# Turning tiles on VectorE and through DRAM instead of on TensorE, with a new order of a planned macaron kernel

## The chip, the cores and the metric

The kernel runs on one core of a Trainium2 chip. The metric is the device time of one launch in microseconds, as the median of several runs; lower is better. The five engines of the core (TensorE or PE for matmuls, VectorE or DVE, ScalarE or ACT, GpSimd or POOL, and SyncE or SP, which here issues all DMAs) run their own instruction streams in order and wait for each other by semaphores.

## What is computed

The input x is 8 sequences of 256 tokens with 128 channels. Six residual layers follow each other, each on a layer-normalized x:

```python
x = x + 0.5 * _L0_ffn_ref(_layernorm(x), ...)   # soft mixture of 16 experts x 64 slots
x = x + _L0_attn_ref(_layernorm(x), ...)        # linear attention, 16 heads, elu + 1
x = x + 0.5 * _L0_ffn_ref(_layernorm(x), ...)   # the soft mixture again
x = x + 0.5 * _L1_ffn_ref(_layernorm(x), ...)   # GLU: silu gate, two hidden layers of 512
x = x + _L1_attn_ref(_layernorm(x), ...)        # attention with FAVOR+ random features
x = x + 0.5 * _L1_ffn_ref(_layernorm(x), ...)   # the GLU again
```

The two attentions, cut to what the change touches:

```python
# L0: out is turned before the last product
out = jnp.einsum('bhnd,bhde->bhne', q, kv) * z
out = jnp.einsum('bnc,oc->bno', out, Wproj) + bproj
# L1: 16 heads x 32 features; phi(q) is turned before num and den
xw = jnp.einsum('bhtd,hmd->bhtm', x, proj)
xw = xw - jnp.max(xw, axis=-1, keepdims=True)
phi = jnp.exp(xw) * jnp.exp(-0.5 * x_norm_sq) + EPS
num = jnp.einsum('bhtm,bhmd->bhtd', phiQ, KV)
den = jnp.einsum('bhtm,bhm->bht', phiQ, Ksum)[..., None] + EPS
```

## The kernel before

All data is float32. x stays in SBUF: 16 tiles of 128 tokens, two to each of the 8 sequences (called blocks, b). The blocks form two groups of four; `group` (L1341) takes one group through the six layers. A product contracts over the partitions, so a normalized tile (tokens on partitions) has to be **turned** to channels on partitions before it can be multiplied with a weight matrix.

Such a turn is a `flip` (L365): a TensorE transpose of a 128x128 tile against the identity into PSUM, followed by a copy to SBUF by ScalarE or VectorE (`evacuated`, L368). `transposed` (L431) turns the tiles of a normalized y: two in `dispatch` of the mixture (with an affine copy), two in `linear` (L877, the first attention) and in `favor` (L1153, the second), four in `glu` (L1088, which takes two blocks at a time). `project` (L848) turns linear attention's output `oh`, two tiles. In `favor`, phi(q) of a block is 128 x 1024: eight flips into two banks, whose copies add the 1e-6 of the features (L1263 to L1271); phi(k) gets its 1e-6 by a GpSimd operation (L1248) and isn't turned.

The mixture's `dispatch` already has another way to turn: its exponentials are transposed by VectorE in 32x32 squares within each group of 32 partitions (L638), which suits products on 32 rows of TensorE at a time. It also spills the normalized tile to DRAM with four DMAs (L539) and spreads it back four times (L546). The weights of the 16 experts are fetched through four buffers `we` (L724, with biases at L727).

Nothing is issued in the order in which it is written. `Plan.step` (L88) records each piece of work with its engines, a duration, its reads and writes and its buffers; `Plan.place` (L121) then puts the steps one after the other on the engines, always the one that can start first, ties broken by a key: the TensorE time recorded so far, plus 45000 for the second group, plus 100 times an entry of the table `SHIFTS` (L16) for its part. A part is a stretch of the program that begins at `plan.part()`; a smaller key is more urgent. Buffers, PSUM banks among them (kind `ps`, eight), are handed out at placing. `Plan.issue` (L199) emits the steps by planned start, so each engine's instruction order is fixed by the plan; at run time the engines wait for semaphores. A step's `lag` is extra time until its result is there; `SP` steps have 2000 ns besides.

At the start, `rehearse` (L1372) multiplies the identity with itself 14 times while the first inputs arrive.

Of the kernel before, what the change touches and what calls it, by code (L numbers as in the profile page):

```python
# [13 lines left out]
P = 128  # L14

SHIFTS = (  # L16
    -1319, -1177, -1179, -234, -76, -310, -312, -70, -340, -338, -86, -385, -231, -437, -534,
    -438, -380, -343, -723, -539, -291, -326, -396, -417, -254, -201, -356, -228, -211, -118,
    -511, -528, 144, 18, -78, 96, 75, -486, -259, 398, 0, 22, 12, -318, -46, 57, 46, 221, -64,
    227, -13, -57, -20, 66, -283, -22, -94, -718, 41, 74, -7, -1, -30, 194, 106, 110, 356, 101,  # L20
    795, 48, -539, 265, -702, -346, -646, -82, 303, -155, 294, 80, -220, -817, 147, -4, 170,
    -282, 25, -136, -36, -246, -35, -196, -181, -374, 25, -551, -218, 387, -155, 231, 607, 1155,
    -140, -62, 4, -209, -206, -92, -131, -189, 63, -176, -155, -174, -142, -353, 51, 69, 141,
    108, 115, 76, 41, 9, -98, -166, -94, 27, -93, -88, -393, -168, -31, 130, -13, -218, -78,
    130, 105, 79, -189, -724, 9, 54, -4219, 183, 328, 534, 422, 1394, 826, 581, -128, 608, -159,
    -23, 92, -24, -186, -220, 25, -168, 774, 492, 254, 433, 585, 230, -113, -207, -80, 377,
    -220, 224, -677, 472, -371, -706, -646, -62, -156, -161, -1077, -2, -479, -102, 119, 36,
    -233, -727, -865, -412, -526, -772, -301, 480, 211, 600, -302, -1825, -1528, 438,
)


# [23 lines left out]
class Step:  # L55
    def __init__(self, number, engines, run, table, key):
        self.number, self.engines, self.run, self.table = number, engines, run, table
        self.key = key
        self.needs, self.feeds, self.bufs = set(), [], []
        self.start = self.end = self.engine = None  # L60


class Plan:
# [57 lines left out]
    def place(self):  # L121

        for s in self.steps:
            s.waiting = sum(n.end is None for n in s.needs)
            for n in s.needs:
                n.feeds.append(s)
        names = list(self.LAG)
        free = dict.fromkeys(names, 800)
        port = 0
        slots = {k: [0] * n for k, n in self.slots.items()}  # L130
        able = {e: [] for e in names}
        table = None
        order = []

        def enable(s):
            s.ready = max((n.end + self.LAG[n.engine] + n.lag for n in s.needs), default=0)
            for e in s.engines:
                able[e].append(s)

        for s in self.steps:  # L140
            if not s.waiting:
                enable(s)
        while len(order) < len(self.steps):
            best = None
            for e in names:
                for s in able[e]:
                    at = max(s.ready, free[e])
                    if e == "POOL":
                        at = max(at, port)
                    elif e == "DVE" and s.port:  # L150
                        at = max(at, free["POOL"])
                    short = {}
                    for b in s.bufs:
                        if b.slot is None:
                            short[b.kind] = short.get(b.kind, 0) + 1
                    for kind, n in short.items():
                        times = sorted(t for t in slots[kind] if t is not None)
                        if len(times) < n:
                            at = None
                            break  # L160
                        at = max(at, times[n - 1])
                    if at is None:
                        continue
                    late = self.TABLE if s.table and s.table != table else 0
                    rank = (at, s.key + 4 * late, s.number)
                    if best is None or rank < best[0]:
                        best = (rank, e, s, at, late)
            if best is None:
                raise RuntimeError("no step can start: too few slots")
            _, e, s, at, late = best  # L170
            for f in s.engines:
                able[f].remove(s)
            s.start, s.engine = at, e
            s.end = free[e] = at + s.engines[e] + late
            if s.table:
                table = s.table
            if e == "DVE" and s.port:
                port = s.end
            for b in s.bufs:
                if b.slot is None:  # L180
                    held = slots[b.kind]
                    b.slot = min(
                        (k for k, t in enumerate(held) if t is not None), key=held.__getitem__
                    )
                    held[b.slot] = None
            for b in s.bufs:
                b.left -= 1
                b.last = max(getattr(b, "last", 0), s.end + self.LAG[e] + s.lag)
                if not b.left:
                    slots[b.kind][b.slot] = b.last  # L190
            order.append(s)
            for n in s.feeds:
                n.waiting -= 1
                if not n.waiting:
                    enable(n)
        self.span = max(free.values())
        self.placed = order

    def issue(self, home):  # L199
        for s in self.steps:  # L200
            for b in s.bufs:
                b.home = home
        for s in sorted(self.placed, key=lambda s: (s.start, s.number)):
            s.run(s.engine)


@with_exitstack
def macaron_kernel(ctx: ExitStack, tc: tile.TileContext, i: dict, out: bass.AP):
# [139 lines left out]
    def ps_(*shape):  # L348
        return Buf("ps", (P, *shape))
# [78 lines left out]
        )  # L428
        return y

    def transposed(y, n, affine=False):  # L431

        pt = ps_(n, P)
        yt = Buf("k1" if n == TT else "k2", (P, n * P))

        def turn(_):
            for t in range(n):
# [409 lines left out]

    def project(b, oh, w):  # L848

        pt = ps_(TT, P)  # L850
        ot = Buf("k1", (P, N))

        def turn(_):
            for t in range(TT):
                flip(pt.ap[:, t, :], oh.ap[:, t, :])

        step({"PE": flips(TT)}, turn, [oh], [pt], takes=[ot])
        evacuated(lambda: ot.ap, lambda: pt.ap.rearrange("p t c -> p (t c)"), [pt], [ot], N)
        projected_onto(b, ot, w)

    def projected_onto(b, ot, w):
# [14 lines left out]

    def linear(b):  # L877
        plan.part()
        yt = transposed(norm(b), TT)
        plus_bias(b, loaded["bproj"])  # L880
        pk, pv = ps_(2, N), ps_(TT, D)
        kq = Buf("k4", (P, 2, 2, N))
# [205 lines left out]
    def glu(b, after):  # L1088
# [7 lines left out]
        y = Buf("k2", (P, 2 * TT, D))  # L1096
        for k in range(2):
            norm(b + k, False, y, k * TT)
        yt = transposed(y, 2 * TT)
        h, to = (Buf("comb", (P, 2, 2, 2, N)) for _ in range(2))  # L1100
        t4 = Buf("comb", (P, 4, 512))
        for o in range(NO):
# [49 lines left out]

    def favor(b):  # L1153
        plan.part()
        yt = transposed(norm(b), TT)
        plus_bias(b, loaded["bo"])
        pq, pv = ps_(2, N), ps_(TT, P)

# [80 lines left out]
        for k in (1, 0):  # L1239
            cells = [(phi, k, c) for c in range(4)]  # L1240

            def exps(_, k=k):
                nc.scalar.activation(phi.ap[:, k], phi.ap[:, k], AF.Exp)

            step({"ACT": act(1024) + 20}, exps, cells, cells, table="exp")
            if k:
                def eps(_, k=k):
                    nc.gpsimd.tensor_scalar(  # L1248
                        phi.ap[:, k], phi.ap[:, k], 1.0, 1e-6, ALU.mult, ALU.add
                    )  # L1250

                step({"POOL": 1100}, eps, cells, cells)

        plan.part()


        qt = lambda t: qk.ap.rearrange("p a b n -> p (a b n)").rearrange(
            "p (t c n) -> p t c n", t=TT, c=4
        )[:, t]
        for t in range(TT):  # L1260
            pt = ps_(4, P)

            def turn(_, t=t, pt=pt):  # L1263
                for c in range(4):
                    flip(pt.ap[:, c, :], phi.ap[:, 0, t, ts(c, P)])

            def finish(e, t=t, pt=pt):
                if e == "ACT":
                    nc.scalar.activation(qt(t), pt.ap, AF.Copy, bias=1e-6)
                else:  # L1270
                    nc.vector.tensor_scalar(qt(t), pt.ap, 1e-6, None, ALU.add)  # L1271

            step({"PE": flips(4)}, turn, [(phi, 0, c) for c in range(4)], [pt])
            step({"ACT": act(512), "DVE": dve(512)}, finish, [pt], [(qk, t)])
        pk, pkt = ps_(2, P), ps_(2, P)
        kvm = Buf("k1", (P, 2, P))

# [91 lines left out]
    )  # L1369
    pwarm = ps_(P)  # L1370

    def rehearse(_):  # L1372
        for _ in range(14):
            mm(pwarm.ap, ident, ident, start=True, stop=True)

    key, plan.key = plan.key, -100000
    step({"PE": 6200}, rehearse, [], [pwarm])
# [8 lines left out]
        nc.tensor.engine, nc.scalar.engine, nc.vector.engine, nc.gpsimd.engine, nc.sync.engine,  # L1386
    }
    with tc.manual_schedule(engines=engines):
        plan.issue(home)


# [62 lines left out]
```

## Time and profile before

| | us |
|---|---|
| median of 3 runs | 758.23 (755.57 to 758.31) |
| the profiled execution | 758.05 |
| its span, first to last instruction | 756.3 |
| TensorE's mean granted clock | 0.995 of full speed |

The groups of instructions that matter here, from the view of groups by shape:

| line, engine, what | count | busy us | mean ns |
|---|---|---|---|
| L747 PE, experts' first products | 512 | 121.0 | 385 |
| L1037 PE, GLU hidden layers | 896 | 205.4 | 381 |
| L366 PE, flips of k tiles | 176 | 34.2 | 284 |
| L366 PE, flips of comb tiles (phi(q)) | 64 | 8.5 | 273 |
| L366 PE, flips of sm tiles | 32 | 5.8 | 278 |
| L373 ACT, copies of 128x256 to k | 25 | 9.2 | 373 |
| L375 DVE, copies of 128x256 to k | 15 | 6.1 | 416 |
| L1269 ACT, copies of turned phi(q) | 11 | 6.3 | 597 |
| L1248 POOL, 1e-6 onto phi(k) | 8 | 8.9 | 1116 |

A float32 matmul is two PE instructions (passes), a flip is one. Busy time of PE is the union of intervals in which some pass is in flight, and passes overlap, so a mean duration is not the distance between two of them. The chain of waits is read for that distance: it follows the work that ended last backwards, so each piece in it lasts as long as it held up the end. Rows that the next section rests on are shown there.

### The profile page before, as it was taken

The page shows a single profiled execution, that of the slowest core. Times are in us where ns is not written, and L with a number is a line of the kernel's source. Part 1 is how long each engine was busy: PE and PEld are TensorE (multiplying, and loading weights), DVE is VectorE, ACT ScalarE, POOL GpSimd, SP SyncE. Part 2 cuts the span into 40 slices and gives each one's busy share as a digit, 9 for nine tenths or more (in the row PEclk, how much of TensorE's full clock was granted, in tenths as well). Part 3 has the DMA queues.
Part 4 walks back from the last instruction along what each step waited for, and adds up shares of the span by engine and source line. Part 5 has one row for each costly group of instructions (what it writes and reads, how often), then busy time and mean ns, then how long its engine had stood idle before and what let it go on. Part 6 is the DMA issues. An engine that isn't in the chain of part 4 may idle for free.

```text
span 756.3 us, 15121 instructions
## 1 busy us (share of the span) xinstructions
PE 738.4 (98%) x5884; PEld 619.5 (82%) x5884; DVE 507.1 (67%) x1084; ACT 432.1 (57%) x815; POOL 294.1 (39%) x404
## 2 busy tenths in 40 slices
PE   7899999999999999999999999999999999999998
PEld 5687888998888988889878788958787896687887
DVE  6986976468988689875453537468875676854432
ACT  4968879756974679873373434146447354644321
POOL 7968318622457444743650201424250151201000
PEclk9999999999999999999999999999999999999999
DMA  5453422224340053323521010000000000000001
GB/s 155 130 156 98 137 92 92 91 82 129 82 145 25 1 143 102 122 91 118 181 72 42 1 49 1 1 1 1 2 1 1 1 1 2 1 1 8 8 1 42
DMA packets 29911, 45.53 MB, mean 60 GB/s; under 512 B 5008, under 2 KB 18704, under 8 KB 29840
## 3 DMA queue, kind: packets, MB, share of 16 engines
q1 hardware_dynamic: 29840, 44.57, 19.6%
q8 instruction: 46, 0.75, 0.4%
q14 instruction: 25, 0.20, 0.1%
HBM read 41.41 MB, written 3.15 MB: 59 GB/s over the span
## 4 chain that ended last, share of the span: by engine, by line
PE 88%; POOL 4%; DVE 3%; DMA 1%; issue 1%; ACT 1%; SPq 1%; ACTq 0%; POOLq 0%; DVEq 0%
PE ps L1037 26%; PE ps L747 14%; PE ps L778 8%; PE ps L651 7%; PE ps L819 6%; PE ps L575 5%; PE ps L1137 4%; PE ps L1107 4%; PE ps L1110 4%; PE ps L366 4%; POOL k L411 1%; POOL sm L405 1%; PE ps L1316 1%; PE ps L1216 1%; PE ps L867 1%
## 5 line engine op out<-in xcount | busy, mean ns | idle before, releaser
L747 PE MATMUL ps<-slots,we 128*128 128x256 f32 x512 | 121.0, 385 | 1.9 <-DMA we<-in_We 1.9
L747 PEld LDWEIGHTS ps<-slots,we 128*128 128x128 f32 x512 | 95.3, 192 | 17.3 <-issue 2.6
L1037 PE MATMUL ps<-comb,slots 128*128 128x256 f32 x448 | 102.8, 381 | 0.0
L1037 PE MATMUL ps<-comb,comb 128*128 128x256 f32 x448 | 102.6, 381 | 0.0
L1037 PEld LDWEIGHTS ps<-comb,slots 128*128 128x128 f32 x448 | 83.4, 190 | 14.5 <-issue 2.2
L1037 PEld LDWEIGHTS ps<-comb,comb 128*128 128x128 f32 x448 | 83.7, 190 | 13.1 <-issue 1.4
L373 ACT COPY k<-ps 128x512 f32<-128x512 f32 (+2 forms) x74 | 36.1, 493 | 87.4 <-PE ps L1037 59.8
L630 POOL TENSOR_TENSOR comb<-comb,sm 128x1024 f32<-128x1024 f32 x32 | 60.6, 1900 | 62.3 <-DVE sm L625 49.8
L697 POOL TENSOR_TENSOR comb<-comb,k 128x1024 f32<-128x1024 f32 x32 | 75.4, 2376 | 22.5 <-ACT k L373 18.3
L753 ACT ACTIVATE k<-ps,small 128x256 f32<-128x256 f32 x128 | 55.1, 475 | 45.1 <-PE ps L747 41.5
L1051 DVE TENSOR_TENSOR comb<-ps,k 128x512 f32<-128x512 f32 x48 | 32.8, 687 | 58.0 <-ACT k L373 31.6
L758 DVE SCALAR_TENSOR_TENSOR k<-ps,small,k 128x256 f32<-128x256 f32 x128 | 56.5, 476 | 20.4 <-ACT k L753 19.9
L617 ACT ACTIVATE comb<-comb,sm 128x256 f32<-128x256 f32 x128 | 63.3, 497 | 5.3 <-DVE sm L609 5.1
L575 PE MATMUL ps<-k,seT 128*128 128x256 f32 x256 | 60.9, 383 | 2.1 <-DVE k L592 0.8
L778 PE MATMUL ps<-we,k 128*64 128x128 f32 x1024 | 61.6, 275 | 0.0
L651 PE MATMUL ps<-comb,k 32*128 32x256 f32 x1024 | 61.4, 387 | 0.0
L778 PEld LDWEIGHTS ps<-we,k 128*64 128x64 f32 x1024 | 55.4, 137 | 7.3 <-issue 3.3
L819 PE MATMUL ps<-slots,comb 128*128 128x129 f32 x512 | 60.4, 276 | 0.0
L403 POOL TENSOR_SCALAR sm<-sm 128x2 f32<-128x2 f32 x52 | 10.1, 194 | 129.0 <-DVE sm L397 118.6
L1059 ACT ACTIVATE comb<-comb 128x512 f32<-128x512 f32 x48 | 30.2, 630 | 51.3 <-DVE comb L1051 51.0
L819 PEld LDWEIGHTS ps<-slots,comb 128*128 128x128 f32 x512 | 58.7, 192 | 1.0 <-issue 0.9
L651 PEld LDWEIGHTS ps<-comb,k 32*128 32x128 f32 x1024 | 52.8, 189 | 6.4 <-issue 2.6
(146 smaller groups left out, 1316.5 us busy)
## 6 DMA issues: line engine op xcount, KB each, us to landing
we<-in_We SPq DMA_DIRECT2D x64, 384.0 KB, 3.9
k<-y SPq DMA_DIRECT2D x64, 128.0 KB, 2.7
y<-k SPq DMA_DIRECT2D x64, 32.0 KB, 1.9
we<-in_bd SPq DMA_DIRECT2D x64, 32.0 KB, 3.6
comb<-in_h2T SPq DMA_DIRECT2D x4, 256.0 KB, 6.9
slots<-in_h1T SPq DMA_DIRECT2D x4, 256.0 KB, 4.5
out<-x SPq DMA_DIRECT2D x8, 128.0 KB, 1.7
x<-in_x SPq DMA_DIRECT2D x3, 256.0 KB, 5.1
```

The source lines that it names most:

```text
L373: nc.scalar.copy(dst(), src())
L575: mm(pl.ap[:, j, :], seT[:, 2 * u + j].rearrange("p k s -> p (k s)"), yt.ap, start=True, stop=True,)
L617: nc.scalar.activation(ex.ap[:, 4 * h + j, :], comb.ap[:, 4 * h + j, :], AF.Exp, bias=mx.ap[:, j : j + 1], accum_out=mx.ap[:, 4 + j : 5 + j],)
L630: nc.gpsimd.tensor_tensor(ex.ap[:, part], ex.ap[:, part], mx.ap[:, 8:12].unsqueeze(2).to_broadcast([P, 4, N]), ALU.mult,)
L651: mm(po.ap, yr.ap[rows, c, :], ex.ap[rows, :, 32 * c : 32 * c + 32], start=(c == 0), stop=(c == N // 32 - 1), tile_position=(32 * a, 0),)
L697: nc.gpsimd.tensor_tensor(raw, raw, mb.ap.unsqueeze(1).to_broadcast([P, 4, N]), ALU.subtract)
L747: mm(pe.ap[:, m, :], we.ap[:, ts(2 * m + c, P)], sl.ap[:, j, k, :, 0:S], start=True, stop=True,)
L753: nc.scalar.activation(ga.ap, pe.ap[:, 0, :], AF.Gelu, bias=bg[:, e, c : c + 1])
L758: nc.vector.scalar_tensor_tensor(ht.ap[:, c, :], pe.ap[:, 1, :], bu[:, e, c : c + 1], ga.ap, ALU.add, ALU.mult,)
L778: mm(po.ap[S * k : S * k + S, q, :], hts[k].ap[:, c, ts(q, S)], wes[k].ap[:, ts(4 + c, P)], start=(c == 0), stop=(c == 1), tile_position=( ...
L819: mm(po.ap[:, t, 0 : D + 1], comb.ap[:, j, ts(t, P)], eo()[:, j, q, 0 : D + 1], start=(j == 0), stop=(j == NJ - 1),)
L1037: mm(bank.ap[:, o], w(k)[:, c, ts(o, P)], rhs().rearrange("p (c n) -> p c n", c=2)[:, c, :], start=(start and o + c == 0), stop=(stop and ...
```

## The change

A new helper, `squares_turned`, turns a piece without TensorE. VectorE transposes it in place in 32x32 squares. One DMA writes the whole piece to a DRAM tile. Four more, one for each group of 32 destination partitions, read the squares back so that each lands where the full transpose wants it; what is moved is runs of 32 floats. It replaces the flips of y in `linear`, `favor` and `glu` (`transposed` with `squares=True`), of linear's output in `project`, and of phi(q) in `favor`. `dispatch` keeps its flips. As no copy is left that could add 1e-6 to phi(q), GpSimd now does it for both phi(k) and phi(q).

`Plan.place` notes where a TensorE step that takes a fresh PSUM bank is planned to start more than 700 ns after TensorE became free, and `Plan.issue` puts identity products into that step's bank ahead of it, one for each 224 ns beyond 300. `SHIFTS` is a new table. In the built program TensorE has 50 identity products (14 of them the old ones); SP issues 497 DMAs.

```diff
 SHIFTS = (
-    -1319, -1177, -1179, -234, -76, -310, -312, -70, -340, -338, -86, -385, -231, -437, -534,
...
+    -1764, -4181, -1024, -349, -26426, -5062, -382, -2111, -1130, -497, 116, -518, -159, 162,
...
 )
...
         self.key = key
         self.needs, self.feeds, self.bufs = set(), [], []
         self.start = self.end = self.engine = None
+        self.idle = 0
 
 
 class Plan:
...
             for f in s.engines:
                 able[f].remove(s)
             s.start, s.engine = at, e
+            before = free[e]
             s.end = free[e] = at + s.engines[e] + late
             if s.table:
                 table = s.table
...
             for b in s.bufs:
                 if b.slot is None:
                     held = slots[b.kind]
+                    if e == "PE" and b.kind == "ps" and not s.idle:
+                        since = max(before, min(t for t in held if t is not None))
+                        s.idle, s.bank = at - since, b
                     b.slot = min(
                         (k for k, t in enumerate(held) if t is not None), key=held.__getitem__
                     )
...
         self.span = max(free.values())
         self.placed = order
 
-    def issue(self, home):
+    def issue(self, home, idle):
+
         for s in self.steps:
             for b in s.bufs:
                 b.home = home
         for s in sorted(self.placed, key=lambda s: (s.start, s.number)):
+            if s.idle > 700:
+                idle(s.bank, int((s.idle - 300) / 224))
             s.run(s.engine)
 
 
...
         )
         return y
 
-    def transposed(y, n, affine=False):
-
+    def squares_turned(z, n, cells, dst, out):
+
+
+        flat = lambda: z()
+        there = dram.tile([P, n // 32, 32], F32, tag=f"t{len(turns)}", name=f"t{len(turns)}")
+        turns.append(there)
+        step({"DVE": 58 + 1.07 * n}, lambda _: nc.vector.transpose(z(), z()), cells, cells)
+
+        def spill(_):
+            nc.sync.dma_start(there.rearrange("p k j -> p (k j)"), z())
+
+
+        def place(_):
+            squares = there.rearrange("(a i) (t f) j -> f i t a j", a=4, f=4)
+            for f in range(4):
+                nc.sync.dma_start(
+                    dst()[32 * f : 32 * f + 32].rearrange("p (t a j) -> p t a j", a=4, j=32),
+                    squares[f],
+                )
+
+        step({"SP": 475}, spill, cells, [there.name], lag=1.5 * n)
+        step({"SP": 2000}, place, [there.name], out, lag=2.5 * n)
+
+    turns = []
+
+    def transposed(y, n, affine=False, squares=False):
+
+        yt = Buf("k1" if n == TT else "k2", (P, n * P))
+        if squares:
+            squares_turned(
+                lambda: y.ap[:, 0:n].rearrange("p t d -> p (t d)"), n * P,
+                [(y, t) for t in range(n)], lambda: yt.ap, [yt],
+            )
+            return yt
         pt = ps_(n, P)
-        yt = Buf("k1" if n == TT else "k2", (P, n * P))
 
         def turn(_):
             for t in range(n):
...
 
     def project(b, oh, w):
 
-        pt = ps_(TT, P)
         ot = Buf("k1", (P, N))
-
-        def turn(_):
-            for t in range(TT):
-                flip(pt.ap[:, t, :], oh.ap[:, t, :])
-
-        step({"PE": flips(TT)}, turn, [oh], [pt], takes=[ot])
-        evacuated(lambda: ot.ap, lambda: pt.ap.rearrange("p t c -> p (t c)"), [pt], [ot], N)
+        squares_turned(
+            lambda: oh.ap.rearrange("p t d -> p (t d)"), N, [oh], lambda: ot.ap, [ot]
+        )
         projected_onto(b, ot, w)
 
     def projected_onto(b, ot, w):
...
 
     def linear(b):
         plan.part()
-        yt = transposed(norm(b), TT)
+        yt = transposed(norm(b), TT, squares=True)
         plus_bias(b, loaded["bproj"])
         pk, pv = ps_(2, N), ps_(TT, D)
         kq = Buf("k4", (P, 2, 2, N))
...
         y = Buf("k2", (P, 2 * TT, D))
         for k in range(2):
             norm(b + k, False, y, k * TT)
-        yt = transposed(y, 2 * TT)
+        yt = transposed(y, 2 * TT, squares=True)
         h, to = (Buf("comb", (P, 2, 2, 2, N)) for _ in range(2))
         t4 = Buf("comb", (P, 4, 512))
         for o in range(NO):
...
 
     def favor(b):
         plan.part()
-        yt = transposed(norm(b), TT)
+        yt = transposed(norm(b), TT, squares=True)
         plus_bias(b, loaded["bo"])
         pq, pv = ps_(2, N), ps_(TT, P)
 
...
                 nc.scalar.activation(phi.ap[:, k], phi.ap[:, k], AF.Exp)
 
             step({"ACT": act(1024) + 20}, exps, cells, cells, table="exp")
-            if k:
-                def eps(_, k=k):
-                    nc.gpsimd.tensor_scalar(
-                        phi.ap[:, k], phi.ap[:, k], 1.0, 1e-6, ALU.mult, ALU.add
-                    )
-
-                step({"POOL": 1100}, eps, cells, cells)
+            def eps(_, k=k):
+                nc.gpsimd.tensor_scalar(
+                    phi.ap[:, k], phi.ap[:, k], 1.0, 1e-6, ALU.mult, ALU.add
+                )
+
+            step({"POOL": 1100}, eps, cells, cells)
 
         plan.part()
 
-
-        qt = lambda t: qk.ap.rearrange("p a b n -> p (a b n)").rearrange(
-            "p (t c n) -> p t c n", t=TT, c=4
-        )[:, t]
-        for t in range(TT):
-            pt = ps_(4, P)
-
-            def turn(_, t=t, pt=pt):
-                for c in range(4):
-                    flip(pt.ap[:, c, :], phi.ap[:, 0, t, ts(c, P)])
-
-            def finish(e, t=t, pt=pt):
-                if e == "ACT":
-                    nc.scalar.activation(qt(t), pt.ap, AF.Copy, bias=1e-6)
-                else:
-                    nc.vector.tensor_scalar(qt(t), pt.ap, 1e-6, None, ALU.add)
-
-            step({"PE": flips(4)}, turn, [(phi, 0, c) for c in range(4)], [pt])
-            step({"ACT": act(512), "DVE": dve(512)}, finish, [pt], [(qk, t)])
+        squares_turned(
+            lambda: phi.ap[:, 0].rearrange("p t c -> p (t c)"), TT * 512,
+            [(phi, 0, c) for c in range(4)],
+            lambda: qk.ap.rearrange("p a b n -> p (a b n)"), [(qk, t) for t in range(TT)],
+        )
         pk, pkt = ps_(2, P), ps_(2, P)
         kvm = Buf("k1", (P, 2, P))
 
...
     )
     pwarm = ps_(P)
 
+    def idle(bank, n):
+        for _ in range(n):
+            mm(bank.home["ps"][bank.slot][:, 0:P], ident, ident, start=True, stop=True)
+
     def rehearse(_):
-        for _ in range(14):
-            mm(pwarm.ap, ident, ident, start=True, stop=True)
+        idle(pwarm, 14)
 
     key, plan.key = plan.key, -100000
     step({"PE": 6200}, rehearse, [], [pwarm])
...
         nc.tensor.engine, nc.scalar.engine, nc.vector.engine, nc.gpsimd.engine, nc.sync.engine,
     }
     with tc.manual_schedule(engines=engines):
-        plan.issue(home)
+        plan.issue(home, idle)
 
 
 def kernel(**inputs):
```

## The prediction

> **What bounds the kernel now.** I read the busy times first, then the chain that ended last, then windows with the granted clock, then the groups by form and the DMA issues.
>
> ```profile
> PE 738.4 (98%) x5884; PEld 619.5 (82%) x5884; DVE 507.1 (67%) x1084; ACT 432.1 (57%) x815; POOL 294.1 (39%) x404
> ...
> PE 88%; POOL 4%; DVE 3%; DMA 1%; issue 1%; ACT 1%; SPq 1%; ACTq 0%; POOLq 0%; DVEq 0%
> ```
>
> TensorE is busy for 738.4 of 756.3 us and is 88% of the chain; no other engine passes 67%. Between 60 us and the tail TensorE idles only some 6 us. So time is TensorE work: what leaves TensorE leaves the span, if no new wait takes its place. The windows show the only stretches in which its clock drops:
>
> ```profile
> 37.00:44.00 7.00, 6.42 (x68) 5.56 (x69) 5.61 (x8) 3.75 (x12) 7.00 (x7) 0.76 0.38 107
> 66.00:72.00 6.00, 6.00 (x23) 4.71 (x22) 2.88 (x7) 3.99 (x7) 6.00 (x4) 0.77 0.02 7
> ```
>
> Columns: stretch, its length, busy us of PE, PEld, DVE, ACT, POOL, then clock, DMA share, GB/s. From 72 us on the clock is 1.00.
>
> **Part 1: flips that leave TensorE.** The order of instructions of both programs has 272 flips before and 128 after. The 144 that go: linear 8 calls x (2 + 2), favor 8 x (2 + 8), glu 8 x 4. Their price where TensorE is dense is read in the chain of waits (start, us, what):
>
> ```profile
> 474.33 1.02 PE ps L366 x8
> ...
> 617.38 1.09 PE ps L366 x10
> ```
>
> That is 128 and 109 ns each (the groups' mean of 284 ns is pipelined latency and would overstate it). 144 x 109 to 128 ns = 15.7 to 18.4 us; I take **-17 us**. After 60 us four waits of TensorE ended at a flip, 3.9 us together; two of them, on a normalized tile (L411, 1.5) and on linear's output (L960, 1.0), may be of the removed kind: -2.5 at best, and I count **-1**.
>
> With the flips go their evacuations: 24 of 256 columns (373 ns on ACT, 416 on DVE) and 24 of 512 (about 590 and 690), some 23 us over two engines with room. Nothing on the path.
>
> **Part 2: what comes instead.** 40 calls of squares_turned: 24 of 256 elements a partition, 8 of 512 (glu), 8 of 1024 (phi(q)). Each is one VectorE transpose, one DMA to DRAM, four DMAs back.
>
> VectorE has the instruction already: 1236 ns for 1024 elements. Scaled, 620 for 512; 256 lies between 310 and its 416 ns copy, I take 340. Sum 8 x 1.24 + 8 x 0.62 + 24 x 0.34 = 23 us, about what the evacuations gave back: VectorE stays near 67%. GpSimd gets the 1e-6 of phi(q): 8 x 1.05 us (row L1248), at 39%. Both are hidden by TensorE's 98%; they cost only as latency inside a turn, below.
>
> The DMA rows:
>
> ```profile
> k<-y SPq DMA_DIRECT2D x64, 128.0 KB, 2.7
> y<-k SPq DMA_DIRECT2D x64, 32.0 KB, 1.9
> ...
> out<-x SPq DMA_DIRECT2D x8, 128.0 KB, 1.7
> ```
>
> The spill of 256 elements is the same transfer as out<-x: 1.7 us. For 1024 I add 384 KB at some 290 GB/s (128 packets of 1 KB of out<-x start within 0.44 us): 3.0 us; for 512, 2.1.
>
> The place is what before does not show: each of its four DMAs writes pieces of 32 floats, 128 B, so 1,024, 2,048 or 4,096 pieces a turn. SP issues such DMAs in 0.42 us (k<-y) to 0.59 (y<-k), so the fourth is issued 1.3 to 1.8 us in, and lands some 2.2 to 2.7 later: 4.2 us if the pieces themselves cost little. What does a piece cost? **Lower end:** the trace's packet records have 13 ns for a 128 B packet (those of projT), 27 for 512 B, 46 for 1 KB; over 16 DMA engines 0.8 ns a piece, 3.3 us for phi(q). **Upper end:** within one y<-k the 64 packets start 4.2 ns apart: 17 us for phi(q). Here a rule speaks against the change. The Trainium skill, "VectorE: DVE Perf Modes", section on the three transpose paths, calls a plain DMA that transposes by access pattern 19 times slower than the crossbar's 1309 ns for a 128x128 tile and sends such turns to TensorE; "DMA: Bandwidth & Descriptors", specifications, wants at least 512 B apiece. Taken by bytes (24.9 us for 32 KB), phi(q)'s 512 KB would cost about 400 us, and the kernel would be several times slower. But the rule's tile moves 16,384 single elements, 1.5 ns each; here VectorE has turned the squares, and 32 floats travel together. By pieces the rule gives 4,096 x 1.5 = 6.2 us. That lies near the row's lower end, so I take **1.6 ns**: 1.6, 3.3 and 6.6 us of transfer, the first hidden under the issues. Place, from first issue to landing: 4.2, 5.3 and 8.3 us.
>
> Now the cover. I counted the TensorE work that the new order puts between the last producer and the first reader of each turn, at the paces of the chain (16 expert products of 256 columns 3.46 us, and so on), and set against it the turn's latency by rows, with about 0.15 us per hand-over:
> - linear's y, 8 turns: add 0.86, statistics 0.89, root 1.08, apply 0.90, turn 0.34, spill 1.7, place 4.2, hand-overs 0.9 = 10.9 us; cover 13.0 to 27.5.
> - linear's output, 8: division 0.95, turn 0.34, spill 1.7, place 4.2, hand-overs 0.6 = 7.8; cover 10.6 to 13.2.
> - favor's y, 8: as linear's, 10.9; cover 12.4 and more.
> - glu, 8: add 0.42, statistics 1.8, root 1.2, apply 1.8, turn 0.62, spill 2.1, place 5.3, hand-overs 0.9 = 14.1; cover 14.5, 15.6, 15.9, 17.2, the rest 19.9 and more.
> - phi(q), 8: four DVE groups of 1.55, table load 1.28, two exps of 1.05, two eps of 1.05 (the first beside an exp), turn 1.24, spill 3.0, place 8.3, hand-overs 0.9 = about 24; cover 24.7, 25.0, 25.3, 26.7, 27.3, 28.2, 29.2, 70.8.
>
> So every turn is covered, the tight ones by 0.3 to 3 us. The sums have no queueing in them: VectorE serves two groups of blocks, and a We fetch of 384 KB (3.9 us to landing) can stand ahead of a place. When that comes on top, TensorE waits. I allow 0.5 us for each of 4 tight glu turns and 7 of phi(q), and 0.1 for the others: **+8 us**, less what overlapping turns share, **+6**. Without any cover a 256 turn alone would add 6 us over a flip and its copy.
>
> SP issues 497 DMAs in place of 297: 200 x 0.42 to 0.59 = 84 to 118 us more. Its queue is in order: behind a place that waits for its spill stand We fetches and other blocks' spills, held for up to 1.7 to 3 us. That they can bear it is seen in SP's own waits:
>
> ```profile
> SPq L724 <- PE ps L778: 158.3, 19, 36.5
> ```
>
> SP stood 158 us at We fetches until TensorE freed a buffer, so it has time; TensorE waited on We once, 1.9 us. Cost in the +6. DMA share: 73,728 pieces x 13 ns / 16 = 60 us, 8% on top of 20%.
>
> **Part 3: idle products and order.** The new order has 36 more identity products, in six batches, all ahead of the first gather of slots (within the first 35 rows of TensorE's order). The 14 of the warm-up took 6.1 us (row L1374), 0.44 each[...]; at the dense pace of two passes of 0.11 us the 36 fill 8 us, and TensorE idled some 6 us in these 44 us before: where a batch outlasts its gap it delays the next flip, up to +3. What they can win: (1 - 0.76) x 7 = 1.7 us of lost clock at 37 to 44; the drop at 66 follows the We wait, where none is put. So -1.7 to +3: **0**, as in most gaps they displace nothing. The rest of the order moves work I can't price by part; it is in the covers above.
>
> **Sum** against the profiled execution (span 756.3, 758.05 with what lies around it; the runs' median is 758.23, so no correction): 758 - 17 - 1 + 6 + 0 = **746 us**, of which I expect 740 to 752.
>
> **Rivals.**
> (a) *Pieces are slow, and phi(q)'s readers wait.* At 4.2 ns its place takes about 19 us, the turn 35, each of seven covers is short by 6 to 10 us, 56 in all; if half overlaps, 28. glu adds about 8. 758 - 18 + 36 to 64 = 776 to 804. For: nothing in before moves such pieces in number, and packets of 512 B start 4.2 ns apart. Against: the records' 13 ns, and the rule's own 1.5 ns. It decides from about 2.8 ns a piece on, where the seven stalls (2.5 us each) eat the 18.
> (b) *SP's order costs the gain in the expert stages.* We fetches and places delay each other, 1 us a linear turn, half shared: +8 on top: 754, 751 to 760. For: each linear turn lies in We traffic (DMA 3 to 5 tenths). Against: the covers there exceed the latencies by 2 to 3 us.
> (c) *Queueing is nil and the clock stays up*: 758 - 18.4 - 2.5 - 1.7 = 735, up to 740.
>
> **Chances.** Forecast 0.60, (a) 0.19, (b) 0.15, (c) 0.06. The range reaches from 737 into (a)'s lower part, 764, leaving out some 0.2. A change under 0.5% (754.4 to 762.0) can't be told from none: faster 0.60 + 0.06 + half of (b) = 0.73; same 0.08; slower 0.19, which is (a).
>
> **What would show it.** TensorE's busy time down by 16 to 18 us with its share still 97% or more; flips 128; clock 1.00 at 37 to 44. Waits of TensorE on DMA k<-t under 1 us each, 6 us together. A landing of phi(q)'s place near 6 to 7 us for the last DMA. Wrong: landings over 10 us there, TensorE idle at products in favor, or waits on We.

## The result

The changed kernel takes 751.84 us (median of 5 runs, 749.39 to 752.22) against 758.23 before: a ratio of 0.9918, 95% interval 0.9891 to 0.9945. It is faster, by about half of the 12 us that were forecast, and just inside the range, whose upper end is 752. The profiled execution took 752.09 us, its span is 750.4.

The page of the changed kernel, busy times and chain:

```profile
PE 730.0 (97%) x5812; PEld 609.8 (81%) x5812; DVE 513.2 (68%) x1094; ACT 419.5 (56%) x782; POOL 316.6 (42%) x425
...
PE 85%; DMA 4%; DVE 2%; SPq 1%; issue 1%; POOL 0%; ACT 0%; DVEq 0%; ACTq 0%; POOLq 0%
```

TensorE still sets the time, but its idle time grew: 750.4 - 730.0 = 20.4 us, where it was 17.9. DMA has 4% of the chain in place of 1%. The stretches with the low clock (same columns as before: stretch, length, busy us of PE, PEld, DVE, ACT, POOL, clock, DMA share, GB/s) and the one where the loss sits, in the changed kernel:

```profile
37.00:44.00 7.00, 6.76 (x97) 5.78 (x99) 5.32 (x7) 4.88 (x15) 6.39 (x6) 1.00 0.22 50
66.00:72.00 6.00, 6.00 (x53) 5.11 (x52) 4.81 (x8) 5.94 (x9) 0.33 (x2) 1.00 0.55 153
150.00:320.00 170.00, 158.54 (x1374) 139.91 (x1372) 132.82 (x312) 107.54 (x219) 77.41 (x116) 0.99 0.44 119
```

The same last stretch in the kernel before:

```profile
150.00:320.00 170.00, 166.72 (x1543) 149.20 (x1542) 141.20 (x326) 122.24 (x261) 83.83 (x115) 1.00 0.31 91
```

The early clock is repaired. Between 150 and 320 us, where both groups' expert stages and linear attention lie, TensorE idles 11.5 us in place of 3.3. From 320 to 700 us it idles 0.2 us in all: the stages with the turns of phi(q) and of the GLU are covered. TensorE's longest waits in the changed kernel (who waited for what, total us, times, longest):

```profile
PE ps L922 <- DMA k<-t: 4.4, 2, 2.4
PE ps L786 <- DMA we<-in_We: 4.4, 3, 2.9
PE ps L989 <- DVE kv L977: 1.9, 1, 1.9
```

L922 reads linear's turned y, L786 is the experts' first product. A wait can cost more than its own length: behind the second wait at L922, 2.4 us up to 192.5, TensorE's granted clock stood at half for 3.4 us, which makes about 1.7 us more. Behind the longest wait on We, 2.9 us up to 307.9, it did not fall. The stretch with the low clock:

```profile
193.60:197.00 3.40, 3.40 (x27) 3.07 (x27) 2.02 (x5) 1.35 (x4) 1.48 (x1) 0.50 0.38 56
```

The chain of waits shows how the first of the two waits at L922 came about (start, us, what):

```profile
165.62 0.61 SPq L454
167.20 3.46 DMA k<-t
170.80 0.68 PE ps L922 x4
```

and SP's own instructions around it:

```profile
161.74 2.59 SPq L454 DMA_DIRECT2D k<-t  x4
164.44 0.53 SPq L448 DMA_DIRECT2D t<-k  x1
165.01 6.74 SPq L454 DMA_DIRECT2D k<-t  x8
171.85 0.55 SPq L763 DMA_DIRECT2D we<-in_We  x1
```

A place is the four DMAs that read a turned piece back, a spill the one that writes it. The first place waits 2.3 us for its spill; then three places, twelve DMAs, go out with one more spill among them, SP is busy issuing for 10 us, and the next We fetch goes out at 171.85. One of the twelve, issued at 167.20, took 1.92 us by itself; it is part of the 3.46 us in the chain. The DMA issues that answer to those shown of before (KB each, median us from issue to landing):

```profile
t<-comb SPq DMA_DIRECT2D x8, 512.0 KB, 2.6
k<-t SPq DMA_DIRECT2D x32, 128.0 KB, 3.4
t<-k SPq DMA_DIRECT2D x24, 128.0 KB, 2.0
k<-t SPq DMA_DIRECT2D x96, 32.0 KB, 2.3
```

From 256 to 1,024 pieces a DMA the landing grows by 1.1 us, with the other three DMAs of the place in flight beside it: 1.4 ns for a piece of one DMA, some 0.4 for a piece of the whole place.

### The profile page after: what moved, and what is told of

It is laid out like the page before. It is cut to its first block, busy times and chain, and to the rows that moved or that the text cites. A ratio compares the mean times of both kernels' runs of the same rounds, so it can differ in the third digit from the quotient of the medians.

```text
span 750.4 us, 15406 instructions
## 1 busy us (share of the span) xinstructions
PE 730.0 (97%) x5812; PEld 609.8 (81%) x5812; DVE 513.2 (68%) x1094; ACT 419.5 (56%) x782; POOL 316.6 (42%) x425
## 4 chain that ended last, share of the span: by engine, by line
PE 85%; DMA 4%; DVE 2%; SPq 1%; issue 1%; POOL 0%; ACT 0%; DVEq 0%; ACTq 0%; POOLq 0%
PE ps L1071 26%; PE ps L786 13%; PE ps L858 7%; PE ps L817 7%; PE ps L690 6%; PE ps L614 4%; PE ps L1171 4%; PE ps L1141 4%; PE ps L1144 4%; DMA we<-in_We 2%; PE ps L374 2%; PE ps L1250 1%; DMA k<-t 1%; PE ps L1335 1%; PE ps L1301 1%; PE ps L901 1%
## 5 line engine op out<-in xcount | busy, mean ns | idle before, releaser
L786 PE MATMUL ps<-slots,we 128*128 128x256 f32 x512 | 119.7, 382 | 4.7 <-DMA we<-in_We 4.4
L786 PEld LDWEIGHTS ps<-slots,we 128*128 128x128 f32 x512 | 94.2, 190 | 22.0 <-DMA we<-in_We 5.0
L1071 PE MATMUL ps<-comb,slots 128*128 128x256 f32 x448 | 104.4, 382 | 0.0
L792 ACT ACTIVATE k<-ps,small 128x256 f32<-128x256 f32 x128 | 57.3, 476 | 42.2 <-PE ps L786 38.2
L381 ACT COPY k<-ps 128x512 f32<-128x512 f32 (+2 forms) x51 | 26.3, 515 | 79.8 <-PE ps L1071 68.1
L817 PEld LDWEIGHTS ps<-we,k 128*64 128x64 f32 x1024 | 56.4, 138 | 8.6 <-issue 3.5
L817 PE MATMUL ps<-we,k 128*64 128x128 f32 x1024 | 62.8, 278 | 0.0
L614 PE MATMUL ps<-k,seT 128*128 128x256 f32 x256 | 61.3, 383 | 1.0 <-ACT seT L528 0.7
```

Of the source, the lines that this page charges most:

```text
L614: mm(pl.ap[:, j, :], seT[:, 2 * u + j].rearrange("p k s -> p (k s)"), yt.ap, start=True, stop=True,)
L786: mm(pe.ap[:, m, :], we.ap[:, ts(2 * m + c, P)], sl.ap[:, j, k, :, 0:S], start=True, stop=True,)
L792: nc.scalar.activation(ga.ap, pe.ap[:, 0, :], AF.Gelu, bias=bg[:, e, c : c + 1])
L817: mm(po.ap[S * k : S * k + S, q, :], hts[k].ap[:, c, ts(q, S)], wes[k].ap[:, ts(4 + c, P)], start=(c == 0), stop=(c == 1), tile_position=( ...
L1071: mm(bank.ap[:, o], w(k)[:, c, ts(o, P)], rhs().rearrange("p (c n) -> p c n", c=2)[:, c, :], start=(start and o + c == 0), stop=(stop and ...
```

## The experiments

Two theories were set against each other. **Q:** the loss is made at SP's queue, where each place takes four issues, with We fetches and other places behind them. **P:** the loss is made on the DMA engines, by the 128 B pieces. A third, **F**, was that the identity products stand in TensorE's way. Runs were made in three groups of four; in each group the kernel before was run on the same chip, with medians of 755.56, 755.25 and 756.56 us. Ratios are to these runs, of means, so they can differ a little from the ratio of the medians. Unless a run says otherwise, the order of work on all compute engines is the changed kernel's.

### First group

Without the fill:

```diff
-            if s.idle > 700:
-                idle(s.bank, int((s.idle - 300) / 224))
```

> The changed kernel (751.8 us) without the 36 identity products in gaps; every other instruction stands in the same order. TensorE's lost time is known by stretch from the trace: to 100 us it is some 2 us less than before the change, from 100 to 310 us some 11 us more. Theory Q (the expert stages lost the gain at SP's queue, the products fill gaps that exist anyway): within 2 us of the changed kernel, with TensorE's clock below 1.00 between 30 and 70 us again, so 752 to 754. Rival F (36 products at 0.22 to 0.44 us stand in TensorE's way and ate 3 to 6 us of the expected gain): 746 to 749.

752.24 us, ratio 0.994 (0.9911 to 0.997): the changed kernel's time. The windows of its first 66 us, and then of the changed kernel's:

```profile
0.00:66.00 66.00, 54.76 (x428) 44.78 (x429) 53.59 (x122) 44.85 (x119) 54.99 (x90) 0.90 0.55 150
```

```profile
0.00:66.00 66.00, 60.41 (x502) 51.26 (x503) 53.70 (x122) 46.25 (x120) 56.43 (x90) 1.00 0.50 140
```

The products bring the clock from 0.90 to 1.00 and busy time up by 5.7 us; in the time of the whole that can't be told from nothing. So F's net loss of 3 to 6 us isn't there; that the products win anything isn't shown either. Two effects may cancel: the runs without the fill reach from 746.82 us at a mean clock of 0.998 to 755.49 at 0.984, while the changed kernel takes 747.81 to 748.21 in those at 1.000 (second group). At an equal clock the products seem to cost 2 to 3 us, an estimate from these runs, and the steadier clock seems to give that back.

One DMA a place, whole rows:

```diff
-            for f in range(4):
-                nc.sync.dma_start(
-                    dst()[32 * f : 32 * f + 32].rearrange("p (t a j) -> p t a j", a=4, j=32),
-                    squares[f],
-                )
+            nc.sync.dma_start(dst(), there.rearrange("p k j -> p (k j)"))
```

> The changed kernel with one DMA for each place in place of four: it reads the spilled rows back as they were written (1 KB to 4 KB a row), so the squares stay on the wrong partitions and what follows works on misplaced values; the same bytes, the same order of all compute engines. SP issues 120 DMAs less, about 73 us of its time at 0.61 us each, and no 128 B pieces are moved. Theory Q (SP's issuing time is what delays places and We fetches): TensorE's waits on DMAs (9.1 us) nearly go, 742 to 747. Theory P (128 B pieces occupy the DMA engines): the same here. If neither holds (the new order or VectorE's part makes the loss): 750 to 753.

739.0 us, ratio 0.9779 (0.9744 to 0.9813). TensorE's waits on DMAs are 1.6 us in all. So the loss comes with the way the places are fetched, but this takes away issues and pieces together.

Four DMAs of whole rows (`dst()[32 * f : 32 * f + 32]` from `rows[32 * f : 32 * f + 32]`):

> As the run with one DMA a place, but four of 32 partitions each, whole rows of 1 KB to 4 KB: as many issues as the changed kernel, no 128 B pieces. The squares stay on the wrong partitions here too. Theory Q: the issues still cost 0.4 to 0.6 us each, so most of the loss stays, 749 to 752. Theory P (pieces on the DMA engines): as fast as with one DMA, 742 to 747.

744.86 us, ratio 0.9848 (0.9802 to 0.9893): between the two, so it decides nothing. It also turned out not to be the test it was meant to be, since the issue itself got shorter (min, median and max ns of one, first and last start). In this run:

```profile
L454 SPq DMA_DIRECT2D k<-t x160: 302/413/1774, 140.7 to 693.2; - x160
```

In the changed kernel:

```profile
L454 SPq DMA_DIRECT2D k<-t x160: 557/612/1920, 140.6 to 699.2; - x160
```

160 issues at 0.2 us less are 32 us of SP's time. What it left are waits on We, 5.2 us.

The kernel before with the new `SHIFTS` alone:

> The kernel before with the new table of shifts alone: flips on TensorE as before, no identity products in gaps, another order. It tells what the new order is worth by itself. If the table is neutral: 755 to 761. If the gain of 6.4 us came from the order and the turns are worth nothing: 750 to 753. If the table only suits the turned version: 762 to 775, with TensorE idle at starts of parts.

806.13 us, ratio 1.0654 (1.0608 to 1.0701). With these steps the table makes a bad layout: between 320 and 500 us TensorE is busy 159.1 of 180 us. The order by itself is worth nothing with flips; what it is worth with the turns isn't known, as they were not run without it.

### Second group

The changed kernel again:

> The changed kernel once more, beside the three others of this group on the same chip: 749 to 753, TensorE waiting some 9 us on DMAs, nearly all of it between 150 and 320 us. If those waits lie at other places in another execution, they are chance and no queue's doing.

749.25 us, ratio 0.9923 (0.9894 to 0.9953). The waits are the same ones: 4.2 us at L922 on k<-t, 3.6 at L786 on We, 1.9 at L989, and TensorE busy for 159.9 us between 150 and 320. They are no chance. The six runs fall into two kinds: at a mean clock of 0.998 to 1.000 they take 747.8 to 750.3 us, at 0.995 they take 752.6 and 752.9.

One DMA a place, but 128 B pieces:

```diff
+            pieces = there.rearrange("p k j -> (p k j)").rearrange("(k p j) -> p k j", p=P, j=32)
+            nc.sync.dma_start(dst().rearrange("p (k j) -> p k j", j=32), pieces)
```

> One DMA for each place as in the run with one DMA (739.0 us), but it reads the spilled squares from 128 B pieces strewn over the DRAM tile; they land on wrong partitions, so what follows works on misplaced values. Same bytes, same number of pieces as the changed kernel, a quarter of its issues. Theory Q (SP's issues make the loss): 739 to 742, near the run with whole rows. Theory P (pieces make it): 746 to 752, near the changed kernel. Both about equally: 743 to 746.

739.74 us, ratio 0.9795 (0.9763 to 0.9827), against 739.0 us and 0.9779 with whole rows: the intervals overlap. Its place DMAs on SP, and TensorE's waits on DMAs:

```profile
L453 SPq DMA_DIRECT2D k<-t x40: 359/372/2918, 140.7 to 688.0; - x40
```

```profile
PE ps L918 <- DMA k<-t: 1.5, 1, 1.5
PE ps L782 <- DMA we<-in_We: 1.3, 2, 1.0
```

The pieces cost nothing that the time shows, and taking three of four issues away (by the medians, 98 us of SP's time become 15) gains 9.5 us against the changed kernel of the same group. P falls.

Two of the four place DMAs on ScalarE's queue, `(nc.sync if f < 2 else nc.scalar).dma_start(`:

> The changed kernel with two of the four place DMAs issued by ScalarE in place of SP: nothing left out. SP gives up 80 issues, some 49 us. ScalarE issues them where the plan has the place, and stands still until the spill has landed (0 to 2 us each, 40 times). Theory Q: the waits of TensorE on We and on places go down by half or more, 744 to 749, unless ScalarE's halts come back as waits on its copies. Theory P: no gain, 751 to 756.

746.62 us, ratio 0.9872 (0.9842 to 0.9901): 2.6 us less than the changed kernel of its group, inside Q's range, but only about a quarter of what one DMA a place gained. TensorE's waits on places and We go from 7.8 to 2.7 us, but new ones on ScalarE and VectorE come (1.3 us each at L614 and L817): ScalarE's halts came back, as Q had allowed.

Linear attention's turns back on TensorE (`transposed(norm(b), TT)`, and `project` as before):

> Linear attention's y and output turned by TensorE again (32 flips, 3.8 us more of TensorE), favor and GLU by squares; the plan lays out anew, so the order changes too. Theory Q with an order that stays good: the 11 us lost in the expert stages come back less 3.8 us, 744 to 748. If the table of shifts suits only the steps it was made for, as the run of flips in the new order (806 us) suggests: 765 and more.

791.34 us, ratio 1.0475 (1.044 to 1.0511). The plan lays out anew and sees long gaps: it puts 187 identity products, 374 passes, where the changed kernel has 50. Like the run with flips in the new order, it tells of the layout and not of the turns.

### Third group

The remedy that Q asks for leaves the turns alone and takes other issues off SP. The biases travel with the weights, behind which they are laid when the inputs are prepared (that line isn't shown):

```diff
-                nc.sync.dma_start(we.ap[:, 0 : 6 * P], i["We"][e])
-                if e % 2 == 0:
-                    for k in range(2):
-                        nc.sync.dma_start(
-                            we.ap[S * k : S * k + S, 6 * P :],
-                            i["bd"][e + k].partition_broadcast(S),
-                        )
+                n = 6 * P if e % 2 else 6 * P + D
+                nc.sync.dma_start(we.ap[:, 0:n], i["We"][e][:, 0:n])
```

> The changed kernel with each pair's biases laid beside the weights in DRAM, so that they come with the We fetch: 64 DMAs of 0.59 us less on SP (38 us, all in the expert stages), the same order on every compute engine, nothing left out. The runs with one DMA a place say SP's issues are the loss. Theory Q: half or more of TensorE's 9 us of waits on DMAs goes, 743 to 747. If only the places' own latency counts, not what stands around them in SP's queue: 748 to 752.

739.7 us, ratio 0.9776 (0.9743 to 0.981), better than Q's own figure: 38 us of SP's time in the expert stages brings as much as one DMA a place, with every place as it was. What is left of TensorE's waits on DMAs is 1.3 us:

```profile
PE ps L781 <- DMA we<-in_We: 0.9, 2, 0.5
PE ps L917 <- DMA k<-t: 0.4, 1, 0.4
```

The spill of `dispatch` in one DMA besides:

```diff
-            for k in range(4):
-                nc.sync.dma_start(
-                    spilled[b].rearrange("i (t k) d -> i k t d", k=4)[:, k],
-                    y.ap[32 * k : 32 * k + 32],
-                )
+            nc.sync.dma_start(spilled[b], y.ap)
...
-                nc.sync.dma_start(yr.ap[32 * a : 32 * a + 32], spilled[b])
+                nc.sync.dma_start(
+                    yr.ap[32 * a : 32 * a + 32].rearrange("p (k t) d -> p k (t d)", k=4),
+                    spilled[b].rearrange("(k i) t d -> i k (t d)", k=4),
+                )
...
-                        po.ap, yr.ap[rows, c, :], ex.ap[rows, :, 32 * c : 32 * c + 32],
+                        po.ap, yr.ap[rows, c % 4 * TT + c // 4, :], ex.ap[rows, :, 32 * c : 32 * c + 32],
```

> The same, and the spill of the mixture's normalized tile in one DMA in place of four, with the squares sorted out as they are read back: 48 DMAs of 0.59 us less besides, 112 in all, 66 us of SP's time, about what one DMA a place saved (73 to 92 us, 739.0 us). Nothing left out. Theory Q: 739 to 744.

737.38 us (737.11 to 737.74), ratio 0.9742 (0.9705 to 0.9779): the best kernel of the study; it leaves nothing out. Its page, its window and its longest waits of TensorE:

```profile
PE 726.6 (99%) x5812; PEld 609.9 (83%) x5812; DVE 512.2 (70%) x1094; ACT 418.0 (57%) x782; POOL 315.5 (43%) x425
```

```profile
150.00:320.00 170.00, 168.48 (x1549) 149.41 (x1550) 140.31 (x329) 118.66 (x254) 86.06 (x121) 1.00 0.43 124
```

```profile
PE ps L780 <- DMA we<-in_We: 0.9, 2, 0.5
PE ps L916 <- DMA k<-t: 0.7, 1, 0.7
```

TensorE idles 9.4 us in all, 1.5 of them between 150 and 320. The places themselves issue and land as slowly as before (612 ns and 2.4 us in the median): what changed is what stands around them. SP's halts at spills aren't the loss by themselves either: the places still wait for their spills, no less than in the changed kernel. First that kernel, then this one (total us, times, longest):

```profile
SPq L454 <- DMA t<-k: 29.6, 19, 3.0
```

```profile
SPq L454 <- DMA t<-k: 33.3, 20, 4.5
```

The two queues on top:

> The same, and two of the four place DMAs on ScalarE's queue. Theory Q: once SP keeps up, nothing is left for the second queue to win, within 2 us of the run with fewer issues; if SP is still behind, down to 737 to 739. ScalarE's halts at places could cost 1 to 3 us instead.

738.63 us, ratio 0.9761 (0.9729 to 0.9793), 1.25 us more than the run before it, and each of its four runs (738.13 to 739.54) is slower than all four of that one: with SP keeping up, a second queue has nothing to win, and costs a little.

The kernel before with the same two savings:

> The kernel before with the same two savings at SP (112 DMAs less). Theory Q says that SP's queue binds only once the turns are in it: before, TensorE waited 1.9 us on We in all and SP stood 158 us at buffers, so 754 to 758, no change. If SP's queue bound before as well: 745 to 751, and the turns' own gain would be smaller than it looks.

753.24 us, ratio 0.9957 (0.994 to 0.9975): a small gain of 3.3 us, a little more than Q expected. It lies in the first 66 us, where TensorE is busy for 57.97 us in place of 55.30; between 150 and 320 us nothing changes (compare 166.72 before):

```profile
150.00:320.00 170.00, 166.62 (x1570) 148.82 (x1572) 143.03 (x325) 120.83 (x265) 82.54 (x111) 1.00 0.31 98
```

So SP's queue did not bind in the expert stages before, and **the change, with SP's queue kept clear on both sides, is worth 753.24 - 737.38 = 15.9 us**. That is 110 ns for each of the 144 flips if all of it is theirs; the new table and the identity products are in it too.

## Why the prediction was right in sign and range, with twice the gain that came

- **144 flips, -17 us, and -1 of waits: borne out in sum.** The pair of runs with fewer issues gives 15.9 for the whole change, table and identity products included, where the two terms make 18. The two waits that the prediction thought removable, 1.5 and 1.0 us, still stand in the kernel before with fewer issues and not in the changed one. So the pace read from the chain, 109 to 128 ns, fits, but no run measures it alone.
- **Evacuations and VectorE at nothing: nothing speaks against it.** VectorE's busy share went from 67 to 68%. A turn of 256 takes 435 ns and one of 512 takes 699, where 340 and 620 were assumed; 1,024 take 1,228.
- **A piece at 1.6 ns: too dear, without harm.** The term stood for each piece of a whole place, 4,096 of them in phi(q)'s. phi(q)'s place took three issues and a landing, 3 x 0.61 + 3.4 = 5.2 us, where 8.3 were assumed; the lower end of its range, 0.8 ns, was nearer. The runs with one DMA a place show no cost of pieces in the kernel's time. phi(q)'s readers never waited, and rival (a) falls with them.
- **Clock and fill at 0: not contradicted.** The early clock was repaired; its worth less the products' cost can't be told from nothing.
- **"Cost in the +6" is the step that failed, in size.** The prediction said of SP "so it has time", from 158 us that it stood at We fetches. The same view of the changed kernel:

```profile
SPq L763 <- PE ps L817: 86.1, 15, 17.2
```

SP still has 86 us of such time. But a total over the run says nothing about a stretch of 10 us in which three places and a spill come together. The covers were set against a turn's own latency, with "no queueing in them", and the allowance for queueing was 0.1 us a linear turn: 16 turns, 1.6 us. Measured, TensorE's idle time between 150 and 320 us grew by 8.2 us, and with SP's queue thinned the time falls by 12 to 14 (from 749.25 and 751.84 to 737.38). Part of the difference is the clock: at half speed for 3.4 us in the changed kernel's trace, and 0.995 to 1.000 over its runs, where the runs with one DMA a place and with fewer issues have 0.999 or 1.000 throughout. Against the kernel before with the same savings, the price of the crowded queue is 15.9 less the 6.0 and 6.4 us that the change brought: some 10 us where +6 stood for everything, and nearly all of it in the expert stages, where least was allowed.
- **Rival (b) had the mechanism**, and its 1 us a linear turn, half shared, was about its size. Its 754 came out too high because the +6 for GLU and phi(q) was kept beneath it, and that didn't come. Its forecast was also the nearer one, 2 us off where the main one was 6 off. That the main range still held the result is in part luck: two errors of opposite sign, too little for linear, too much for phi(q) and the GLU, left 751.84 just below 752.
- **The signs it named.** The clock at 37 to 44 us came as said. Not so TensorE's busy time: it fell by 8.4 us where 16 to 18 were named; of the difference the identity products, busy themselves, hide some 3 (726.8 us without them, 730.0 with). Waits on places under 1 us each didn't hold, with one of 2.4, and waits on We were named as a sign of being wrong: they came, with 4.4 us.

What stays open: whether SP's usual issuing time alone holds the queue up, or also the single issues that took up to 1.92 us, one of which stands in the chain shown. Such issues are there without the loss too (up to 2.92 us with one DMA a place and pieces, 1.56 with fewer issues), so they aren't enough by themselves; what makes them long wasn't tried. Nor was the new table tried on its merits: both runs that put flips into it lose their layout.

## What to carry to other kernels

An in-order queue that issues DMAs is an engine like the others: count its issues by the stage and not over the run, with what stands behind each wait, before a plan puts more of them in. When a round trip through memory looks too slow, take away its issues and its pieces one at a time; here a quarter of the issues with the same pieces gave nearly all of the loss back (9.5 of some 10 us). The cheapest remedy can be to thin out what else uses the queue, which leaves the change itself as it is.

## What the runs showed of the hardware

SP's time for a DMA depends on its pattern far more than on its bytes, in medians: 326 ns for 128 rows of 4 KB, 372 for 128 rows in runs of 128 B, 413 for 32 whole rows, 612 for 32 rows in runs of 128 B. Runs of 128 B from DRAM cost little: 13 ns a packet on one of 16 DMA engines, and no time of the kernel that shows in the pair of runs with one DMA a place (739.0 us with whole rows, 739.74 with runs). A wait of TensorE can cost more than it lasts: after one of 2.4 us the granted clock was 0.50 for 3.4 us, though after another of 2.9 us it stayed at 1.00. And, of the planner and not of the hardware, a layout from a greedy plan is brittle: the same table of shifts that takes 752 us with one set of steps takes 791 and 806 with two others.
